# A two-layer graph network in one kernel: which product opens pass 1, and products in the last tile's waits that nothing reads

## The chip, the cores and the metric

The kernel runs on one NeuronCore of one Trainium2 chip. The metric is the device time of one execution in microseconds, lower is better; the figure given for a kernel is the median of several executions. Before the change it is 2499.7 us, the median of 3 executions (2497.94, 2499.7 and 2507.48). A profile was taken in one more execution, which took 2495.86 us; its span from the first to the last instruction is 2494.1 us, and all times inside the profile count from the start of that span.

## The reference

The input `x` has 128 graphs of 64 nodes with 768 features each; `adj` is a 0/1 matrix of 64 x 64 for each graph. Two residual layers follow each other. Everything is float32. Cut to what matters:

```python
# layer 0
h = relu(layernorm(x))
ctx = (adj @ (h @ Wadj.T + badj)) / deg + (adj.T @ (h @ Wrev.T + brev)) / rdeg + h @ Wself.T + bself
rel = (sum over j of adj[i,j] * E[rels[i,j]]) @ Wr.T + ...   # and the same for the reverse direction
x = x + ctx + rel
# layer 1: graph attention with 6 heads of 128
h = relu(layernorm(x))
hh = h @ W[head]                                     # 768 -> 6 x 128
a = leaky_relu(tanh(hh) @ w_src + (tanh(hh) @ w_dst).T)
a = softmax(where(adj == 0, -999, a))
f = elu(a @ hh + b)
g = sigmoid(h @ H_w.T + H_b)
x = x + g * f + (1 - g) * h
```

## The kernel before

Two graphs fill the 128 partitions of a tile, so there are 64 tiles (`NT`), taken in 32 pairs (`NP`). Pass 1 computes layer 0 for all pairs, one pair after the other. Pass 2 then computes layer 1 for all pairs.

The large products of a pair are a 2 x 3 by 3 x 3 product of blocks (2 tiles, 3 thirds of the features). From pair 1 on they are done with 15 block products of sums in place of 18 plain ones. Each row of the table names the left and the right factor, the PSUM bank (`a` to `d`), whether the product begins a new sum in that bank, the output block that is then read out of the bank, the sign of the reading, and whether the relation terms (`counts`) are added into the bank first:

```python
PRODUCTS = (
    ("f1", "g6", "a", True, "11", "+", False),
    ("f7", "g10", "b", True, "00", "-", False),
    ("a01", "b11", "d", True, "01", "+", True),
    ("f4", "b21", "a", False, "01", "-", False),
    ("a00", "g12", "b", False, "01", "-", False),
    ... (8 rows cut)
    ("a11", "g1", "b", False, "11", "+", True),
    ("f2", "g11", "a", False, "10", "+", True),
)
PLAIN = tuple((f"a{k}{j}", f"b{j}{q}", "abcdab"[2 * i + k], j == 0, ...   # pair 0 alone
```

In pass 1 a bank is a tile of its own with one buffer (`pwa` to `pwd` in the profile), so a product that begins a new sum in it waits until VectorE has read what stood there before. A product is six float32 matmuls of 128 x 256, shown as twelve in the profile. Behind the 15 products stands one block of relation terms alone, in bank `d`:

```python
        def main(p):
            bank = {}
            def new(b):
                bank[b] = psw.tile([P, 512], F32, name=f"pw{b}")      # psw: bufs=1
            def counts(b, c, first=False):                            # 2 bf16 matmuls (L617)
                ...
            def add(b, c, sign="+"):                                  # VectorE reads the bank
                k, q = int(c[0]), int(c[1])
                v = X[2 * p + k][:, q * CQ : (q + 1) * CQ]
                if sign == "+":
                    nc.vector.tensor_add(v, bank[b][:, :CQ], v)       # L625
                else:
                    nc.vector.tensor_sub(v, v, bank[b][:, :CQ])       # L627
            def product(an, bn, b, first, c, sign, cnt):
                ...                                                   # matmuls: L633; then counts, add
            for x in PRODUCTS if p else PLAIN:
                product(*x)

            rest_of = ["12"] if p else ["00", "10"]
            for i, c in enumerate(rest_of):
                b = "dc"[i % 2]
                steps.append(lambda b=b, c=c: (counts(b, c, True), add(b, c)))
```

Beside these steps stand, at fixed places, the other work of a pair: the sums `f1` to `f11` (the factors, formed on VectorE, L305 and L307), the preparation of the next pair, and the normalisation of the pair before. `f5`, `f6` and `f3` of a pair are formed right at its start; `f10` after 10 of its steps (six steps are one product).

In pass 2 the instructions stand in two written lists, `ORDER` for the steady part and `END` for the last pairs; each engine runs its own in that order. The parts of the attention that the change touches or that stand near it:

```python
        def rows(t):                                  # "rows": the two attention vectors, as rows
            PS[t] = pss.tile([P, 512], F32, name="ps")              # pss: three buffers
            nc.tensor.matmul(PS[t][:NR, : N + P], sdb[t % 2]..., idr, start=True, stop=True)   # L966
        def rows_dst(t):                              # "rrow"
            nc.vector.tensor_mul(rrow[t % 2][: 2 * HB], PS[t]..., de[: 2 * HB])                # L970
        def rows_src(t):                              # "lrow"
            nc.scalar.copy(lrow[t % 2][2 * HB :], PS[t][2 * HB : NR, N : N + P])               # L975
        def logits(t):                                # "log"
            PS[t] = pss.tile([P, 512], F32, name="ps")[:, : H * N].rearrange("p (h n) -> p h n", h=H)
            nc.tensor.matmul(PS[t], lrow[t % 2], rrow[t % 2], start=True, stop=True)           # L983
        def choose(t):                                # "cp": where adj, on VectorE            # L987
        def turn_p(t):                                # "turnp": 3 transposes of exp(...)      # L1014
        def attend(t):                                # "att": 24 matmuls of 64 x 128          # L1032
        def divide(t, r):                             # "ev": over the sum, into FF[t], VectorE, L1042
            if t not in FF:
                FF[t] = work.tile([P, D], F32, name="f")            # work: two buffers
        def store(t):                                 # "dma": FF[t] added into the output, from GpSimd
            nc.gpsimd.dma_start(of[t * P : (t + 1) * P, :], FF[t], accum_op=OP.add)            # L1067
```

`PG10` to `PG14` are the last five products of the last pair for the gate (half as wide as elsewhere, L1099), and `RG10` to `RG14` are their readings on VectorE (L1114, L1116). The part of `END` about them is

```python
END = """
... (cut)
pre0 f0.0/1 PG11 RG7 f0.1/1 k1 ev1.0/1 ev1.1/1 tr0 RG9 e1/1 chain1 exp0.0 rows1 f0.2/1 RG11
lrow1 rrow1 log1 swap1 exp0.1 f1.0/1 PG10 RG8 cp1 pre1 f1.1/1 tr1 turnp0 swap0 rec0 pT0 exp1.0
f1.2/1 att0 exp1.1 RG10 PG12 dma0/1 ev0.0 ev0.1 e0.0 rec1 RG12 f0.0.0 PG13 RG13 f0.1.0 e0.1
... (cut)
"""
```

where a step with `/1` belongs to the pair before the last, and a step without it to the last pair (`rows1` and `log1` are thus those of the last tile, tile 63).

Of the kernel before, what the change touches and what calls it, by code (L numbers as in the profile page):

```python
# [8 lines left out]
F32 = mybir.dt.float32  # L9
# [6 lines left out]
P = 128  # L16
# [37 lines left out]
# [6 lines that stand above are left out]
    ("f3", "g8", "c", True, "12", "-", False),  # L60
    ("a02", "g14", "a", False, "00", "-", False),
    ("f9", "g9", "b", False, "02", "+", False),
# [10 lines left out]
PLAIN = tuple((f"a{k}{j}", f"b{j}{q}", "abcdab"[2 * i + k], j == 0, f"{k}{q}" if j == 2 else None,  # L73
               "+", i > 0) for i, q in enumerate((0, 2, 1)) for k in range(2) for j in range(3))
# [58 lines left out]
def kernel(  # L133
# [45 lines left out]
    nc = tc.nc  # L179
    G, N, D = x.shape  # L180
# [5 lines left out]
    H, DO = w_src.shape  # L186
    T = G * N
    NT = T // P
    GT = P // N
    NP = NT // 2  # L190
# [35 lines left out]
    def merged(main, side):  # L226

        side = sorted(side, key=lambda e: e[0])
        i = 0
        for n, step in enumerate(main):  # L230
            while i < len(side) and side[i][0] <= n:
                side[i][1]()
                i += 1
            step()
        for _, step in side[i:]:
            step()
# [117 lines left out]
    with ExitStack() as px:  # L354
# [3 lines left out]
        pss = px.enter_context(tc.tile_pool(name="pss0", bufs=2, space=bass.MemoryType.PSUM))  # L358
# [245 lines left out]
        def main(p):  # L604

            bank = {}
            steps = []

            def new(b):
                bank[b] = psw.tile([P, 512], F32, name=f"pw{b}")  # L610

            def counts(b, c, first=False):
                k, q = int(c[0]), int(c[1])
                if first:
                    new(b)
                for i, (a, e) in enumerate(PARTS):
                    nc.tensor.matmul(bank[b][:, :CQ], CT_T[p, k][: 3 * (e - a), i, :],  # L617
                                     tabs[i][:, q * CQ : (q + 1) * CQ],
                                     start=(first and i == 0), stop=True, skip_group_check=True)

            def add(b, c, sign="+"):
# [8 lines that stand above are left out]
                def step(q, s):  # L630
                    if first and q == s == 0:
                        new(b)
                    nc.tensor.matmul(  # L633
                        bank[b][:, :CQ], OPS[p, an][:, q, s, :],
                        bw[bn][:, (s * KQ + q) * CQ : (s * KQ + q + 1) * CQ],
                        start=(first and q == s == 0), stop=(q == KQ - 1 and s == 2),
                        skip_group_check=True)
                    if q == KQ - 1 and s == 2 and c:
                        if cnt:
                            counts(b, c)  # L640
                        add(b, c, sign)
                for q in range(KQ):
                    for s in range(3):
                        steps.append(lambda q=q, s=s: step(q, s))

            for x in PRODUCTS if p else PLAIN:
                product(*x)

            rest_of = ["12"] if p else ["00", "10"]
# [3 lines that stand above are left out]
            return steps  # L653
# [144 lines left out]
        for p in range(NP):  # L798
            merged(main(p), beside(p) if p else first)
# [3 lines left out]
    with ExitStack() as px:  # L803
# [3 lines left out]
        pss = px.enter_context(tc.tile_pool(name="pss1", bufs=3, space=bass.MemoryType.PSUM))  # L807
# [24 lines left out]
        de = wb.tile([P, H, N], BF16, name="de")  # L832
        nc.gpsimd.tensor_copy(de, dl[:, :, None].to_broadcast([P, H, N]))

        idr = wb.tile([P, N + P], BF16, name="idr")
# [84 lines left out]
        def hz(t):  # L920
            return (hzs[t % NHZ][:, 0, :].rearrange("p (h o) -> p h o", h=H), hzs[t % NHZ][:, 1, :])

        TH, PR, SD, SG, PS, AM, AL, PB, DN, MX, PT, PO, FF, EE, HX = ({} for _ in range(15))
# [32 lines left out]
        def swap(t):  # L956

            hx = HX[t] = work.tile([P, H, DO], F32, name="hx")
            for g in range(GT):
                nc.sync.dma_start(hx[g * N : (g + 1) * N], hz(t)[0][(1 - g) * N : (2 - g) * N])  # L960

        def rows(t):


            PS[t] = pss.tile([P, 512], F32, name="ps")
            nc.tensor.matmul(PS[t][:NR, : N + P], sdb[t % 2].rearrange("p c v -> p (c v)")[:, :NR],  # L966
                             idr, start=True, stop=True)

# [10 lines left out]
            nc.gpsimd.memset(AM[t], NEG_MASK / LEAKY)  # L979

        def logits(t):
            PS[t] = pss.tile([P, 512], F32, name="ps")[:, : H * N].rearrange("p (h n) -> p h n", h=H)
            nc.tensor.matmul(PS[t], lrow[t % 2], rrow[t % 2], start=True, stop=True)  # L983

        def choose(t):
# [80 lines left out]
        def store(t):  # L1066
            nc.gpsimd.dma_start(of[t * P : (t + 1) * P, :], FF[t], accum_op=OP.add)  # L1067

        OF_TILE = {
            "th": tanh, "mul": multiply, "k": own_graph, "chain": split, "swap": swap, "rows": rows,  # L1070
            "rrow": rows_dst, "lrow": rows_src, "memset": fill,
            "log": lambda t: (load_x(t), logits(t)), "cp": choose, "pre": leaky, "tr": largest,
            "rec": one_over, "turnp": turn_p, "pT": copy_p, "att": attend, "g": gate, "e": exp_f,
            "dma": store,
# [161 lines left out]
```

## Time and profile before

| | us |
|---|---|
| median of 3 executions | 2499.7 |
| span of the profiled execution | 2494.1 |
| TensorE (PE) busy | 2458.7 (99%) |
| TensorE weight loads (PEld) busy | 1724.9 (69%) |
| VectorE (DVE) busy | 1998.9 (80%) |
| ScalarE (ACT) busy | 1074.4 (43%) |
| GpSimd (POOL) busy | 449.2 (18%) |
| mean granted TensorE clock | 0.998 of full speed |

A row of the chain or of a group names the line of the kernel, the engine, the operation and its operands as output<-inputs; behind it stand the times. In a list in order of time the first number is the start in us from the start of the span, the second the time taken, and a bracket at the end tells how long the engine had been idle before it and what ended that. Matmuls are pipelined: the time shown for one includes its way through the array, and the next may start before that is over, so the cost of a matmul in a row of them is read from one start to the next. Pass 1 runs from the start to about 1505 us, pass 2 from there to the end.

### The profile page before, as it was taken

The numbers are of one execution on the slowest core, as the hardware profiler recorded it, in microseconds if no ns is written. First come the engines' busy times: TensorE is split into PE (matmuls) and PEld (weight loads), VectorE is DVE, ScalarE is ACT, GpSimd is POOL, SyncE is SP. The second block draws the span as 40 slices with busy tenths as digits, with TensorE's granted clock in tenths as the row PEclk, the third lists the DMA queues.
The fourth block names the chain that finished last, engine by engine and source line by source line (L and its number), as shares of the span: only waits on it lengthen the run. The fifth ranks groups of instructions, "written<-read, shape, count | busy, mean of one in ns | idle before, by whom it ended". The sixth has DMA issues, their size and how long they took to land. (4 is left out here: it accounts for less than half of the span.)

```text
span 2494.1 us, 35435 instructions
## 1 busy us (share of the span) xinstructions
PE 2458.7 (99%) x12108; PEld 1724.9 (69%) x12108; DVE 1998.9 (80%) x4105; ACT 1074.4 (43%) x3591; POOL 449.2 (18%) x799
## 2 busy tenths in 40 slices
PE   8999999999999999999999999999999999999997
PEld 6888888888888888888888884444444444444445
DVE  8877777777777777777777766888888888888889
ACT  2122122122122222222222224777777777777777
POOL 1112112112111121121121121111111111111122
PEclk9999999999999999999999999999999999999999
DMA  5112112112122122122122154344444444444434
GB/s 178 55 53 106 53 60 100 53 66 93 54 72 87 53 74 85 53 79 81 54 88 72 53 174 140 94 110 111 109 104 110 104 104 104 107 113 105 104 85 100
DMA packets 116215, 224.58 MB, mean 90 GB/s; under 512 B 36554, under 2 KB 49981, under 8 KB 116034
## 3 DMA queue, kind: packets, MB, share of 16 engines
q1 hardware_dynamic: 106162, 197.50, 24.4%
q0 software_dynamic: 9728, 24.78, 6.2%
q8 instruction: 95, 1.56, 0.3%
q14 instruction: 86, 0.70, 0.1%
q10 hardware_dynamic: 144, 0.04, 0.0%
HBM read 96.07 MB, written 100.66 MB: 79 GB/s over the span
## 5 line engine op out<-in xcount | busy, mean ns | idle before, releaser
L633 PE MATMUL pwa<-weights,op 128*128 128x256 f32 x2304 | 548.9, 383 | 10.6 <-DVE x L625 8.8
L633 PEld LDWEIGHTS pwa<-weights,op 128*128 128x128 f32 x2304 | 417.4, 190 | 79.3 <-DVE x L625 17.3
L633 PE MATMUL pwb<-weights,op 128*128 128x256 f32 x1536 | 360.7, 381 | 0.0
L633 PEld LDWEIGHTS pwb<-weights,op 128*128 128x128 f32 x1536 | 289.1, 190 | 44.9 <-issue 6.7
L889 PE MATMUL pma<-weights,op_f 128*128 128x512 f32 x620 | 307.7, 593 | 0.6 <-DVE weights L916 0.6
L286 POOL TENSOR_TENSOR rn<-ve,mhalf 128x1 f32<-128x1 f32 x128 | 93.7, 732 | 948.6 <-DVE ve L285 948.5
L307 DVE TENSOR_TENSOR op<-op 128x768 f32<-128x768 f32 x248 | 241.3, 993 | 1.2
L941 ACT ACTIVATE pr<-pr 128x128 f32<-128x128 f32 x768 | 225.4, 296 | 25.3 <-DVE pr L931 25.2
L483 ACT ACTIVATE h<-x,rn 128x768 f32<-128x768 f32 x64 | 62.4, 1022 | 399.8 <-DVE rn L290 380.9
L663 ACT ACTIVATE hf<-x,rn 128x768 f32<-128x768 f32 x64 | 65.7, 1027 | 353.7 <-issue 250.1
L594 ACT COPY op<-pb 128x768 f32<-128x768 f32 x160 | 121.1, 797 | 180.9 <-PE pb L586 180.3
L889 PE MATMUL pmb<-weights,op_f 128*128 128x512 f32 x372 | 191.2, 595 | 0.0
L889 PEld LDWEIGHTS pma<-weights,op_f 128*128 128x128 f32 x620 | 111.8, 190 | 113.2 <-issue 104.3
L633 PE MATMUL pwc<-weights,op 128*128 128x256 f32 x780 | 187.0, 383 | 0.0
L633 PE MATMUL pwd<-weights,op 128*128 128x256 f32 x768 | 176.3, 379 | 0.0
L633 PEld LDWEIGHTS pwc<-weights,op 128*128 128x128 f32 x780 | 145.6, 190 | 25.2 <-issue 6.7
L665 POOL TENSOR_TENSOR x<-x,hf 128x768 f32<-128x768 f32 x64 | 136.1, 2127 | 134.9 <-ACT hf L663 134.9
L633 PEld LDWEIGHTS pwd<-weights,op 128*128 128x128 f32 x768 | 145.8, 190 | 20.0 <-issue 0.2
L586 PE MATMUL pb<-r,h 64*128 64x192 f32 x1536 | 151.8, 337 | 0.4 <-ACT h L483 0.4
L625 DVE TENSOR_TENSOR x<-pwa,x 128x256 f32<-128x256 f32 x95 | 40.0, 422 | 134.2 <-PE pwa L617 78.4
L586 PEld LDWEIGHTS pb<-r,h 64*128 64x128 f32 x1536 | 122.9, 187 | 33.9 <-issue 22.7
L941 ACT ACTIVATION_READ_ACCUMULATOR pr<-pr 128x1 f32 x768 | 144.4, 188 | 0.0
(207 smaller groups left out, 4337.6 us busy)
## 6 DMA issues: line engine op xcount, KB each, us to landing
x<-in_x_dram SPq DMA_DIRECT2D x64, 384.0 KB
h<-hf SPq DMA_DIRECT2D x64, 384.0 KB
out_dram<-x SPq DMA_DIRECT2D x64, 384.0 KB
hh<-hh SPq DMA_DIRECT2D x64, 384.0 KB
h<-h SPq DMA_DIRECT2D x64, 384.0 KB
x<-hh SPq DMA_DIRECT2D x64, 384.0 KB
out_dram<-f POOLq DMA_DIRECT2D x62, 384.0 KB, 5.0
hx<-weights SPq DMA_DIRECT2D x88, 192.0 KB
```

The source lines that it names most:

```text
L286: nc.gpsimd.tensor_tensor(to[:, 0:1], ve, mhalf, op=OP.pow)
L307: return (nc.vector.tensor_add if s1 == "+" else nc.vector.tensor_sub)(to, x, y)
L483: nc.scalar.activation(h, X[t], AF.Relu, scale=to[:, 0:1], bias=to[:, 1:2])
L586: nc.tensor.matmul(ps[:, g, i * 3 * N : (i + 1) * 3 * N], H0[t][s, kb * P : (kb + 1) * P], rts[p % 2][s, k].rearrange("p s n -> p (s n)"), ...
L594: nc.scalar.copy(a.rearrange("p h s (g n) -> p g (h s) n", g=GT), ps[:, :, : 6 * N].rearrange("p g (x n) -> p g x n", n=N))
L625: nc.vector.tensor_add(v, bank[b][:, :CQ], v)
L633: nc.tensor.matmul(bank[b][:, :CQ], OPS[p, an][:, q, s, :], bw[bn][:, (s * KQ + q) * CQ : (s * KQ + q + 1) * CQ], start=(first and q == s ...
L663: nc.scalar.activation(h, X[t], AF.Relu, scale=to[:, 0:1], bias=to[:, 1:2])
L665: nc.gpsimd.tensor_add(X[t], X[t], h)
L889: nc.tensor.matmul(bank[p, b], OPS[p, an][:, q, :], bw2[bn][:, 2 * q * CQ : 2 * (q + 1) * CQ], start=(first and q == 0), stop=(q == KQ - 1 ...
L941: nc.scalar.activation(PR[t][:, j, h, :], PR[t][:, j, h, :], AF.Copy, accum_out=to)
```

## The change

It has two parts, which do not depend on each other.

In pass 1, from pair 1 to pair 30, the first two products change places: the one into bank `b` comes first, the one into bank `a` second. Pair 31, the last, keeps the old order, and pair 0 has products of its own. The reason for it: the last product of a pair ends in bank `a`, and so did the next pair's first begin there.

In pass 2, for the last tile alone, TensorE gets nine products ahead of the matmul of `rows` and twelve ahead of that of `logits`, each of a bf16 identity with a constant of 384 columns, into the PSUM tile that the real matmul then overwrites. Nothing reads them. They are meant to keep TensorE working through two waits, so that its clock stays at full speed for the work behind.

```diff
-            for x in PRODUCTS if p else PLAIN:
+            later = (PRODUCTS[1], PRODUCTS[0], *PRODUCTS[2:]) if p + 1 < NP else PRODUCTS
+            for x in later if p else PLAIN:
                 product(*x)
@@
+        def keep_awake(t, n):
+            for i in range(n if t == NT - 1 else 0):
+                nc.tensor.matmul(PS[t][:, : H * N], idr[:, N:], de.rearrange("p h n -> p (h n)"),
+                                 start=True, stop=True)
+
         def rows(t):
             PS[t] = pss.tile([P, 512], F32, name="ps")
+            keep_awake(t, 9)
             nc.tensor.matmul(PS[t][:NR, : N + P], sdb[t % 2].rearrange("p c v -> p (c v)")[:, :NR],
                              idr, start=True, stop=True)
@@
         def logits(t):
-            PS[t] = pss.tile([P, 512], F32, name="ps")[:, : H * N].rearrange("p (h n) -> p h n", h=H)
+            PS[t] = pss.tile([P, 512], F32, name="ps")
+            keep_awake(t, 12)
+            PS[t] = PS[t][:, : H * N].rearrange("p (h n) -> p h n", h=H)
             nc.tensor.matmul(PS[t], lrow[t % 2], rrow[t % 2], start=True, stop=True)
```

## The prediction

> **What bounds the kernel now.** I first read the page's busy times, then who waits for whom on TensorE in pass 1, then one change of pairs in order of time.
>
> ```profile
> PE 2458.7 (99%) x12108; PEld 1724.9 (69%) x12108; DVE 1998.9 (80%) x4105; ACT 1074.4 (43%) x3591; POOL 449.2 (18%) x799
> ```
>
> TensorE is the bound nearly everywhere: 99% busy, and the next, VectorE, at 80%. A shorter pass 1 can come only from TensorE's gaps. Its waits between 100 and 1510 us are listed next (engine and line, what it waited for, us in total, times, longest), for the matmuls and for the weight loads.
>
> ```profile
> PE pwa L633 <- DVE x L625: 8.8, 30, 0.3
> PE pwa L633 <- DVE x L627: 1.7, 1, 1.7
> ...
> PEld pwa L633 <- DVE x L625: 17.3, 30, 0.6
> ```
>
> Thirty equal waits, one at each change of pairs from pair 2 to pair 31, all for VectorE's reading of bank `a`. The single wait of 1.7 us is at 1501.9, inside pair 31, which keeps its order. One change of pairs in order of time:
>
> ```profile
> 717.60 0.39 PE L617 MATMUL pwb<-tab,cntT 126*128 126x256 bf16 x2
> ...
> 718.03 0.42 DVE L625 TENSOR_TENSOR x<-pwb,x 128x256 f32<-128x256 f32 x1 [2.09 <-PE pwb L617]
> ...
> 720.81 0.38 PE L617 MATMUL pwd<-tab,cntT 126*128 126x256 bf16 x2
> 721.01 0.42 DVE L625 TENSOR_TENSOR x<-pwa,x 128x256 f32<-128x256 f32 x1 [2.56 <-PE pwa L617]
> 721.35 0.41 DVE L625 TENSOR_TENSOR x<-pwd,x 128x256 f32<-128x256 f32 x1
> ...
> 721.49 2.86 PE L633 MATMUL pwa<-weights,op 128*128 128x256 f32 x12 [0.29 <-DVE x L625]
> ```
>
> Bank `a` is read from 721.01 to 721.43, and the next pair's first product starts at 721.49. Bank `b` had been read by 718.45, over 2.5 us before it could be wanted. For what the row would look like without a wait, the only change of pairs that has none, from pair 0 to pair 1:
>
> ```profile
> 72.95 0.38 PE L617 MATMUL pwd<-tab,cntT 126*128 126x256 bf16 x2
> 73.17 0.39 PE L617 MATMUL pwc<-tab,cntT 126*128 126x256 bf16 x2
> 73.39 2.75 PE L633 MATMUL pwa<-weights,op 128*128 128x256 f32 x12
> ```
>
> A pair of relation matmuls costs 0.22 us from start to start, and the product behind it starts at once.
>
> The other part lies in the last 25 us. The columns after the stretch are its length, then busy time and instructions of PE, PEld, DVE, ACT and POOL, then TensorE's granted clock and the DMA's share and rate.
>
> ```profile
> 2470.00:2472.00 2.00, 0.16 (x1) 0.00 (x0) 2.00 (x8) 1.16 (x6) 1.32 (x6) 1.00 0.84 202
> 2472.00:2474.60 2.60, 0.28 (x1) 0.21 (x2) 2.32 (x6) 2.55 (x11) 0.21 (x1) 1.00 0.25 98
> 2474.60:2477.00 2.40, 2.36 (x8) 1.68 (x7) 2.40 (x4) 1.06 (x5) 0.69 (x1) 0.58 0.56 55
> 2477.00:2480.00 3.00, 2.43 (x30) 1.98 (x30) 2.39 (x8) 2.50 (x13) 0.87 (x1) 0.77 0.47 87
> ```
>
> TensorE idles from 2470.2 to 2474.6 but for one matmul, and then gets 0.58 and 0.77 of its clock. VectorE is busy nearly throughout. Its one stop there, in order of time:
>
> ```profile
> 2474.39 0.90 POOL L1067 DMA_DIRECT2D out_dram<-f  x1 [2.40 <-DVE weights L1114]
> ...
> 2479.45 1.64 DVE L1042 SCALAR_TENSOR_TENSOR f<-ps,dn,bb 128x128 f32<-128x128 f32 x6 [0.61 <-DMA out_dram<-f]
> ```
>
> The stop ends with a transfer: `f` has two buffers, and tile 62's division writes the one whose store (tile 60's) was issued at 2474.39.
>
> **What the skill says.** "TensorE: Matmul & The Clock Gate", part 1 (the HAM clock gate): TensorE's clock falls to half after an idle window of about 3.4 us, and rises again after as long a busy one; the window runs freely. The trace agrees in kind: 0.58 follows 4.4 us of near idleness, and in order of time the slow stretch runs from about 2474.6 to 2478, some 3.4 us. The same page, "Architectural detail", says that TensorE's queue can pull weight loads ahead of running matmuls. The trace agrees: after a change of pairs with a wait the first twelve matmuls take 2.69 us to the next product's first (721.49 to 724.18), with no wait 2.59 (73.39 to 75.98); the missing 0.10 is a weight load that stood exposed. "Perfetto Trace Analysis", "Identifying the Most-Contended Engine", warns that matmul busy time is a poor metric because matmuls are pipelined. Here 99% busy hides these waits: the 0.29 us shown as idle is only part of what one costs, which is why I read starts.
>
> **The change in pass 1.** It removes and adds no instruction. With no wait the first product would start 0.22 after 720.81, at 721.03; it starts at 721.49. So a change of pairs loses 0.46 + 0.10 = 0.56 us.
>
> - Pairs 2 to 30 now open in bank `b`, free since 718.45: 29 x 0.56 = 16.2 us gained.
> - Pair 1 loses. Pair 0's own list ends in bank `b`, and VectorE, late with the sums, reads it only from 73.34. As above (read from 721.01, product at 721.49) the product can start 0.48 later, at 73.82 in place of 73.39: 0.43, and 0.10 for the restart, 0.5 us lost.
> - Pair 31 keeps bank `a` first and its 0.56.
>
> The sum is 16.2 - 0.5 = 15.7 us, all on TensorE, which sets the end of pass 1.
>
> Does a new wait take its place? The second product now needs bank `a` at 721.03 + 2.59 = 723.62; it is free at 721.43. The fourth product needs bank `a`'s second reading. That product now ends at 726.2, VectorE is through `f10` at 726.3 (shown there in the kernel before), reads by about 726.85, and the fourth product comes at 729.59 - 0.56 = 729.03: 2.2 us spare. Bank `b`'s reading, behind the forming of `f5`, `f6` and `f3` (until 724.45), is done by 724.9 and wanted at 731.7. VectorE has 578.3 us of work in the 770 us from 700 to 1470, so 34.8 in a pair of 46.3 us; 45.7 is enough. The operand buffers turn in the old order (17 buffers, 16 taken in a pair); those of `f1` and `f7` are taken again only in the last third of the pair.
>
> Pass 2 shifts forward as a whole; from 1700 to 2300 us TensorE was busy for 600.00 of 600 us.
>
> **The change at the end.** In the changed kernel's order the nine products stand behind `PG11`, the twelve behind the matmul of `rows`. A product of 384 bf16 columns costs about 0.16 us from start to start (L983 at 2474.64, the next at 2474.80). Nine are 1.5 us, from about 2470.0 to 2471.5, and the real matmul can't start before its operand at 2472.0: 0.5 us spare. Twelve are 2.0 us, to about 2474.1, and `rrow` comes at 2474.6: 0.5 spare. Their PSUM tiles are free by then (readings ended at 2468.2 and 2471.8). So they cost nothing, and TensorE stays busy enough to keep its clock.
>
> What full speed would bring TensorE: `PG10` takes 1.57 us on the chain, 0.86 elsewhere; the three transposes behind it 0.65 or so in place of 0.33; the 24 attention matmuls about 1.2 in place of 0.8. That is 0.7 + 0.3 + 0.4 = 1.4 us. But on the path that sets the end little of it counts. The copy behind the transposes must also wait for ScalarE's work on tile 63 (until about 2476.9). The attention would end near 2478.2 in place of 2479.0, and the division behind it waits for the store until 2479.4 either way. From there VectorE runs to 2490 with stops of at most 0.33 us, in a fixed order. I take 0.1 us for this part.
>
> **The sum.** 15.7 + 0.1 = 15.8 us. From the median of 2499.7 that gives 2483.9. The profiled execution took 2495.86 and one of three 2507.48, so that the median may stand a little high; I say 2483.5.
>
> **The rivals.**
>
> 1. *The wait only moves.* VectorE reads late somewhere after the change, or another bank takes over. For it: VectorE is 80% busy, in order, and already made pair 31 wait for 1.7 us. Against it: the spare 2.2 us above, and some 10 us of VectorE's idleness in a pair. It would leave 2495 to 2500.
> 2. *The waiting part alone counts.* If only the displayed idle time of 0.29 us comes back, 28 x 0.29 = 8 us, time 2491. Against it stand the starts; it is the size to which I would fall back.
> 3. *The end counts in full.* If the store lands earlier than I think, or the executions before had the slow clock longer, 1.4 us more, time 2482.
> 4. *The unread products get in the way.* At half clock twelve would take 4 us and put off `logits` by about 1.5 us. Against it: the clock was 1.00 up to 2474.6. Time 2485.5.
>
> **Range and chances.** The mechanism of pass 1 repeats 29 times with the same numbers, so most of the width is the spread of the executions (0.4% from lowest to highest before). The range is 2477 to 2491. A gain of 2% would be 50 us, more than all of TensorE's gaps in pass 1, and a loss of 2% needs a new wait of about 1.7 us in each pair: faster 0.01, same 0.98, slower 0.01.
>
> **What would show it.** The list of TensorE's waits should have one row of about 0.3 us for bank `a` (pair 31) and one for bank `b` (pair 1) where there were thirty. A pair should take 45.74 us in place of 46.30, the last matmul of pass 1 should come near 1489 in place of 1505, and the clock should be 1.00 from 2470 to 2482 less the shift, with VectorE's stop for the store still there. I would be wrong if pairs still took 46.3, if a wait for `a` or `b` appeared at the third or fourth product, or if the span from the end of pass 1 to the end changed by over 0.5 us.

## The result, and the profile after

In the session that compares the two kernels the changed one takes 2480.08 us (median of 4 executions, 2479.78 to 2481.04) and the one before 2501.7 (4 executions, 2497.94 to 2507.48): a ratio of 0.9912 [0.9891, 0.9933]. That is within 2%, 3.4 us under the predicted 2483.5, and inside the range.

The medians differ by 21.6 us, but the two profiled executions by 2495.86 - 2480.07 = 15.8, which is the predicted sum to a tenth. So there are two questions: is each part of the 15.8 what I said it is, and where do the other 5.8 come from? The first line of the page, after:

```profile
PE 2453.2 (99%) x12129; PEld 1725.8 (70%) x12129; DVE 1998.8 (81%) x4105; ACT 1074.3 (43%) x3591; POOL 449.0 (18%) x799
```

TensorE has 21 instructions more, the unread ones, and is still the bound. Its waits for VectorE from 60 to 1500 us (engine and line, what it waited for, us in total, times, longest):

```profile
PE pwa L633 <- DVE x L627: 1.8, 1, 1.8
...
PE pwa L633 <- DVE x L625: 0.3, 1, 0.3
PE pwb L633 <- DVE x L625: 0.3, 1, 0.3
```

Thirty waits for bank `a` have become one (pair 31, old order) and one for bank `b` (pair 1). The single long wait near the end of pass 1 is still there. The same change of pairs as in the prediction, in order of time:

```profile
713.81 0.39 PE L617 MATMUL pwd<-tab,cntT 126*128 126x256 bf16 x2
...
714.01 0.42 DVE L625 TENSOR_TENSOR x<-pwa,x 128x256 f32<-128x256 f32 x1 [2.56 <-PE pwa L617]
714.03 2.75 PE L633 MATMUL pwb<-weights,op 128*128 128x256 f32 x12
...
716.62 2.75 PE L633 MATMUL pwa<-weights,op 128*128 128x256 f32 x12
...
719.42 0.42 DVE L625 TENSOR_TENSOR x<-pwa,x 128x256 f32<-128x256 f32 x1 [0.19 <-PE pwa L633]
```

The first product starts 0.22 us after the last relation matmuls and takes 2.59 to the next product, as it does where nothing waits. Bank `a`, read until 714.43, is wanted at 716.62. Its second reading ends at 719.84, and the fourth product wants it at 722.03: 2.2 us spare, the predicted figure. Over 16 pairs the same relation matmuls lie (1445.65 - 713.81) / 16 = 45.74 us apart, against (1461.61 - 720.81) / 16 = 46.30 before.

Pair 1 and the end of pass 1, in order of time on TensorE (the second part lies 1413 us later):

```profile
72.92 0.39 PE L617 MATMUL pwc<-tab,cntT 126*128 126x256 bf16 x2
73.57 2.86 PE L633 MATMUL pwb<-weights,op 128*128 128x256 f32 x12 [0.27 <-DVE x L625]
...
1485.98 2.86 PE L633 MATMUL pwa<-weights,op 128*128 128x256 f32 x12 [1.79 <-DVE x L627]
1488.67 0.39 PE L617 MATMUL pwa<-tab,cntT 126*128 126x256 bf16 x2
...
1489.12 0.38 PE L868 MATMUL ps<-ident,h 128*128 128x128 f32 x2
```

Pair 1's first product starts 0.65 after the relation matmuls in place of 0.22, a loss of 0.43, and 0.11 for the restart (2.70 to the next product in place of 2.59). The first matmul behind pass 1's products comes at 1489.12; before it came at 1505.04. Of the 15.92 us between, 0.25 were there before pair 1 began (72.92 against 73.17), so the exchange made 15.67.

The last tile, in stretches that answer to those of before, shifted with the work (columns as there):

```profile
2454.00:2456.00 2.00, 1.72 (x11) 0.78 (x8) 2.00 (x8) 1.16 (x7) 1.32 (x6) 1.00 0.84 196
2456.00:2458.70 2.70, 2.23 (x13) 1.29 (x14) 2.41 (x6) 2.65 (x11) 0.30 (x2) 1.00 0.29 109
2458.70:2461.00 2.30, 1.52 (x8) 1.12 (x7) 2.30 (x4) 1.04 (x5) 0.68 (x1) 1.00 0.51 41
2461.00:2464.00 3.00, 2.46 (x31) 2.13 (x32) 2.46 (x8) 2.57 (x13) 0.87 (x1) 1.00 0.53 99
```

TensorE is busy in the first two, and the granted clock (the first column behind POOL's) is 1.00 in all four, where before it was 0.58 and 0.77 in the last two. In order of time on TensorE, and then VectorE's stop:

```profile
2454.09 1.63 PE L969 MATMUL ps<-de,idr 128*128 128x384 bf16 x9
2456.13 0.28 PE L977 MATMUL ps<-idr,sdb 128*82 128x192 bf16 x1 [0.42 <-POOL sdb L955]
2456.25 2.11 PE L969 MATMUL ps<-de,idr 128*128 128x384 bf16 x12
2458.73 0.32 PE L996 MATMUL ps<-rrow,lrow 82*128 82x384 bf16 x1 [0.37 <-DVE rrow L981]
2458.89 1.03 PE L1112 MATMUL pmb<-weights,op_f 128*128 128x256 f32 x4
```

```profile
2463.47 1.64 DVE L1055 SCALAR_TENSOR_TENSOR f<-ps,dn,bb 128x128 f32<-128x128 f32 x6 [0.54 <-DMA out_dram<-f]
```

The unread products end 0.42 and 0.37 us before the operands of the real ones come, `PG10` takes 0.86 us to the next start (the transposes, at 2459.75) in place of 1.53 (2476.33 - 2474.80 before; the prediction's 1.57 is the chain's figure), and VectorE still stops for the store of tile 60. (The rows with x9 and x12 are the unread products; the real matmul follows each.) From 1489.12 to the end these two profiles take 989.18 us, against 989.06 from 1505.04 before. So in them the second part brought nothing, as predicted. The experiments show that this holds for these two profiles only.

### The profile page after: what moved, and what is told of

Its sections match the earlier page's. It is cut to its first block, busy times and chain, and to the rows that moved or that the text cites. A ratio compares the mean times of both kernels' runs of the same rounds, so it can differ in the third digit from the quotient of the medians.

```text
span 2478.3 us, 35477 instructions
## 1 busy us (share of the span) xinstructions
PE 2453.2 (99%) x12129; PEld 1725.8 (70%) x12129; DVE 1998.8 (81%) x4105; ACT 1074.3 (43%) x3591; POOL 449.0 (18%) x799
```

## The experiments

**What is to be told apart.** Theory A (mine): the exchange is worth 15.7 us by the starts, and the end next to nothing. Its first rival: only the displayed idle time counts, 8 us. The second: the end is worth 1 to 2 us, because executions differ in where the slow clock falls, and the one that I read was a lucky one. The third asks for the other 5.8 us: something in the change that the profiles don't show, or differences between executions in places that the change doesn't touch.

Each time below is the median of a kernel's executions, with lowest, highest and number; each ratio is to the kernel before in the same session, where that took 2500.45 (23 executions, 2496.49 to 2504.63), 2498.81 (11) and 2499.09 (16). The record names another chip for each of these three sessions, so a kernel is compared with the one before in its own session.

**The kernel before against itself.** No edit.

> The kernel before itself, for its spread and for one more profile. Theory A (all of the gain lies in 29 changes of pairs, and the rest of the difference of the medians, 21.6 against 15.8 in the profiles, is spread of the kernel before between executions): the profiled span is again 2494 to 2496 us, or, if it is one of the longer executions, the extra time is found in one place that has nothing to do with the change of pairs. Theory C (in other executions VectorE's reading of bank a comes later than in the profiled one, so the change of pairs costs more than 0.56): a longer execution shows waits for bank a of over 0.3 us.

2502.14 us (2495.91 to 2504.39, 12), ratio 1.0004 [0.9994, 1.0014]. Its profiled execution took 2503.52, 7.7 us longer than that in the prediction, with the same instructions. The first place where they part is the start, on TensorE in order of time; first this execution, then the one in the prediction:

```profile
11.34 2.85 PE L458 MATMUL pb<-wrt,es 128*81 128x384 f32 x4
...
18.47 3.68 PE L633 MATMUL pwa<-weights,op 128*128 128x256 f32 x8
```

```profile
10.88 1.52 PE L458 MATMUL pb<-wrt,es 128*81 128x384 f32 x4
...
14.62 1.99 PE L633 MATMUL pwa<-weights,op 128*128 128x256 f32 x8
```

Every matmul takes nearly twice as long, until about 22 us, with no wait between. Pair 0's last relation matmuls in bank `b` come at 78.26 in place of 72.72: 5.54 us lost. (The views show the granted clock as 1.00 here in both, because the trace has no record of it ahead of its first rise. That first record, at full speed, begins at 21.91 us here and at 10.55 in the prediction's profile, which agrees with the durations.) The second place is the last tile. Stretches as above, then three stops of VectorE in order of time:

```profile
2478.30:2480.50 2.20, 0.00 (x0) 0.10 (x1) 1.91 (x5) 2.15 (x12) 0.23 (x1) 0.77 0.26 103
2480.50:2483.00 2.50, 2.48 (x8) 1.93 (x7) 2.50 (x5) 1.04 (x5) 0.68 (x1) 0.50 0.55 61
2483.00:2486.00 3.00, 2.43 (x27) 1.75 (x26) 2.12 (x6) 2.47 (x13) 0.88 (x1) 0.50 0.44 80
...
2489.00:2490.00 1.00, 1.00 (x6) 0.91 (x5) 0.69 (x2) 0.07 (x1) 0.00 (x0) 0.63 0.00 0
```

```profile
2485.59 1.64 DVE L1042 SCALAR_TENSOR_TENSOR f<-ps,dn,bb 128x128 f32<-128x128 f32 x6 [0.88 <-PE ps L1032]
...
2487.60 0.42 DVE L1116 TENSOR_TENSOR weights<-weights,pma 128x256 f32<-128x256 f32 x1 [0.27 <-PE pma L1099]
...
2489.31 0.42 DVE L1114 TENSOR_TENSOR weights<-pmb,weights 128x256 f32<-128x256 f32 x1 [0.82 <-PE pmb L1099]
```

The same wait of TensorE, but the slow clock starts before the work comes and lasts longer: a clock of 0.77 in the first stretch is half speed for 46% of it, so from 2479.5, and 0.63 in the last is full speed for its last 26%, so until 2489.7. `PG10`, the transposes, the attention, `PG12` and `PG13` all lie in these 10.2 us. VectorE stops for TensorE three times, 1.97 us in all, where in the prediction's profile it stopped for the store alone. From the start of `PG11` (2475.01) to the start of VectorE's last two instructions (2496.90) it takes 21.89 us, there 20.10. The waits for bank `a` are the same 30 of 0.3 us, 8.8 in all, so theory C, a later reading in the longer executions, doesn't hold. Theory A wanted the extra time in one place; it lies in two, and 0.3 us of it in a third, below.

**The exchange alone.** `keep_awake` makes nothing.

> Only the exchange of the first two products, no unread products at the end. Theory A: span 2478.3 +- 0.3, time 2480 to 2482, within 1 us of the changed kernel; TensorE's clock in the last 20 us falls again as it did before. Theory B (the unread products bring the 6 us by which the medians differ more than the profiles): time about 2486.

```diff
-            for i in range(n if t == NT - 1 else 0):
+            for i in range(0):
```

2484.62 us (2483.27 to 2489.86, 4), ratio 0.9941 [0.9926, 0.9956]: 15.8 us under the session's median of before. That is neither theory A's 2480 to 2482 nor theory B's 2486, so the time alone decides nothing; the profile does. The last tile took 21.85 us, with the clock at 0.50 from 2461 to 2470, as in the kernel before against itself. Against the changed kernel's 20.03 the lack of the unread products cost 1.8 us here. The profile showed a third place where executions differ, the wait near the end of pass 1: 3.10 us where the changed kernel's profile has 1.79, and the twelve matmuls behind it 4.38 to the next start in place of 2.69, at half clock.

**The end alone.** The old order in all pairs, with the unread products.

> Only the unread products, the old order of products. Theory A: span within 0.3 us of 2494.1 in a profile of the same kind, clock 1.00 through the last tile, no change of the time beyond the spread of the kernel before. Theory B: about 6 us less than the kernel before. A third possibility, that the end counts in full: 1.4 us less in the span.

```diff
-            later = (PRODUCTS[1], PRODUCTS[0], *PRODUCTS[2:]) if p + 1 < NP else PRODUCTS
+            later = PRODUCTS
```

2499.47 us (2495.76 to 2503.87, 12), ratio 0.9993 [0.9984, 1.0002]. By the medians alone this can't be told from nothing: the executions lie 8 us apart. The profile tells it, the last tile took 19.81 us. It also has the pass-1 wait at its worst, on TensorE in order of time:

```profile
1503.23 5.49 PE L633 MATMUL pwa<-weights,op 128*128 128x256 f32 x12 [3.04 <-DVE x L627]
1508.52 0.63 PE L617 MATMUL pwa<-tab,cntT 126*128 126x256 bf16 x2
```

These twelve matmuls take 5.29 us from start to start.

**All pairs but pair 1.** Pair 1 keeps the old order, pair 31 gets the new one.

> The changed kernel, but pair 1 has the old order and pair 31 the new one. Theory A: pair 1 gets its 0.5 us back (no wait for bank b at its start). Pair 31 loses its wait of 0.3 us at the start, but further on VectorE waits for loads of the weights of pass 2 and TensorE for VectorE (1.8 us near the end of pass 1), so that the 0.56 us saved there comes back as a longer wait of 2.3 us. Sum: span 0.5 us below the changed kernel's 2478.3. If pair 31 counts too: 1.1 us below.

```diff
-            later = (PRODUCTS[1], PRODUCTS[0], *PRODUCTS[2:]) if p + 1 < NP else PRODUCTS
+            later = (PRODUCTS[1], PRODUCTS[0], *PRODUCTS[2:]) if p > 1 else PRODUCTS
```

2484.75 us (2482.85 to 2487.87, 4), ratio 0.9939 [0.9924, 0.9953]. This was a miss on my side, and it shows what pair 31's exception is for. Pair 31 on TensorE:

```profile
1445.59 2.75 PE L633 MATMUL pwb<-weights,op 128*128 128x256 f32 x12
1448.18 0.59 PE L633 MATMUL pwa<-weights,op 128*128 128x256 f32 x2
1451.68 2.43 PE L633 MATMUL pwa<-weights,op 128*128 128x256 f32 x10 [2.91 <-DMA weights<-in_w_cat_dram]
```

In the last pair the first weights of pass 2 are loaded at its seventh step, into the place of `g6`, which by then has been read if `f1` x `g6` is the first product. As the second it reads the new weight: TensorE waits 2.91 us for the load, and pair 31's blocks are computed with a replaced factor. The time is to be read with that. Pair 1 itself starts without a wait there (73.17, then 73.39), as in the kernel before. Up to the end of pair 30, which the replaced factor doesn't touch, this profile has the 29 changed openings by themselves: the last relation matmuls of pair 30 come at 1445.37 us, in the prediction's profile at 1461.61, and those of pair 0 in the same bank `d` at 72.95 in both. That is 16.24 us, 0.56 for each.

**The changed kernel against itself**, in a second session. No edit.

> The changed kernel again, beside the two next ones. By the profiles so far three stretches differ between executions by the phase of TensorE's clock: the first 25 us (the first products run at half clock for up to 5 us longer), the wait near the end of pass 1 (1.7 to 3.1 us, and after the long ones 12 products at half clock, up to 2.6 us more), and, without the unread products, the last tile (20.1 or 21.9 us from the last product before the wait to VectorE's last instruction; 19.8 to 20.0 with them). So the time is 2479 to 2488 from execution to execution, ratio to the kernel before 0.993, that is 15.7 us of pass 1 and 1 to 1.8 of the end. If it is 2480 throughout, ratio 0.991, the exchange calms more than the end.

2488.05 us (2482.88 to 2488.84, 6), ratio 0.9947 [0.9933, 0.9960]. So the same kernel that took 2479.8 to 2481.0 before takes up to 8 us more here, and the difference of medians is 10.8 us in place of 21.6. The profiled execution (2483.64) had the pass-1 wait at 3.42 us and 4.38 for the twelve matmuls, 3.3 us more than in the first profile, and its usual start (72.92). Four others took 2487.7 to 2488.8; they were not profiled, and which place made them long is not shown.

**Three sums later.** The wait near the end of pass 1 is VectorE's: in pair 31 it forms sums of pass 2's weights, some of which wait for loads, and it takes its instructions in order. On VectorE, changed kernel, in order of time:

```profile
1480.51 2.48 DVE L307 TENSOR_TENSOR weights<-weights 128x1024 f32<-128x1024 f32 x2 [1.35 <-DMA weights<-in_hw_t_dram]
...
1485.51 0.41 DVE L627 TENSOR_TENSOR x<-x,pwa 128x256 f32<-128x256 f32 x1
```

The reading at 1485.51, for which TensorE waits, stands behind them. The edit moves three of them back, so that the two that stood ahead of this reading stand behind it:

> The changed kernel; in pair 31 three sums of weights of pass 2 (g1, g8, g11) stand on VectorE behind the readings of banks a and b that they stood in front of. If the wait of 1.7 to 3.1 us near the end of pass 1 is VectorE's order (the readings stuck behind sums that wait for loads), it goes, and with it the half clock after it: 1.7 us less in a good execution, 2.5 to 4 less in the median. If the loads themselves set the end of pass 1, the wait moves to the first products of pass 2 and the time is unchanged.

```diff
-                    (59, "g5"), (65, "v"), (67, "g3"), (70, "g9"), (73, "g1"), (76, "g8"),
-                    (79, "g11"))])
+                    (59, "g5"), (65, "v"), (67, "g3"), (70, "g9"), (78, "g1"), (84, "g8"),
+                    (84, "g11"))])
```

2479.03 us (2478.07 to 2484.44, 6), ratio 0.9918 [0.9904, 0.9933]. The wait fell to 0.55 us, with the clock kept:

```profile
1490.28 2.86 PE L633 MATMUL pwa<-weights,op 128*128 128x256 f32 x12 [0.55 <-DVE x L627]
```

How long the wait is, a load decides. VectorE's last sum ahead of the readings waits for a part of `hw_t` to land, 1.3 to 3.5 us in the profiles, and TensorE's wait follows it. With the sums in their old place it is 0.42 to 0.45 us longer than VectorE's in seven of eight profiles (from 1.33 and 1.75 in the prediction's to 2.99 and 3.42 in the changed kernel's second); the eighth, the exchange alone, has 2.38 and 3.10. With the three sums later it is 1.4 to 1.8 us shorter than VectorE's: 1.94 leaves 0.55 here, and in kernels below 2.67 leaves 1.14 and 3.46 leaves 1.71. So the edit shortens the wait and takes it away only when the load comes early. Why the load lands later in one execution than in the next is not shown.

The executions fall into two groups, 2478.1 to 2479.5 (four) and 2483.9 to 2484.4 (two). The median is 9.0 us under that of the changed kernel in the same session; that is more than this wait can give, and the changed kernel's four long executions are in it. The profiled one is of the second, and its matmuls at the start ran at half speed as in the kernel before against itself: pair 0's relation matmuls came at 78.46, 6 us later than the changed kernel's 72.47.

**Unread products at the start.** Sixteen small ones ahead of TensorE's first matmul and fifteen ahead of its next group, into PSUM tiles that the real ones then overwrite.

> The changed kernel; TensorE gets 16 unread products before its first one and 15 in its second wait (2.4 to 6.4 us from the start), which the real ones then overwrite. If the spread of the start (pair 1 begins at 72.4 to 78.3 us) is the clock's window, the clock is up by 9 us in each execution: pair 1 begins at 71 to 72.5 us, and the longest executions lose up to 5.5 us, the median 1 to 3. If loads set the start, nothing changes.

```diff
@@ ahead of TensorE's first matmul
-            ds = pss.tile([P, 2, 512], F32, name="pb")[:, 0, : 4 * N].rearrange(
-                "p (k d n) -> p k d n", k=2, d=2)
+            pb = pss.tile([P, 2, 512], F32, name="pb")
+            for i in range(0 if p else 16):
+                nc.tensor.matmul(pb[:, 0, :P], blkb, blkb, start=True, stop=True)
+            ds = pb[:, 0, : 4 * N].rearrange("p (k d n) -> p k d n", k=2, d=2)
@@ ahead of the first table product
+                for j in range(15):
+                    nc.tensor.matmul(TAB["ps"][:, 0, :P], blkb, blkb, start=True, stop=True)
```

2480.81 us (2479.72 to 2482.40, 5), ratio 0.9923 [0.9910, 0.9936]. The start on TensorE:

```profile
2.36 1.89 PE L520 MATMUL pb<-blkb 128*128 128x128 bf16 x16 [2.36 <-DVE blkb L404]
...
4.40 1.80 PE L457 MATMUL pb<-blkb 128*128 128x128 bf16 x15
6.71 2.82 PE L460 MATMUL pb<-wrt,es 128*81 128x384 f32 x4 [0.50 <-DVE mv L283]
...
10.77 1.52 PE L460 MATMUL pb<-wrt,es 128*81 128x384 f32 x4
```

The clock is not up by 9 us, as I had expected it to be: its first record begins at 10.24 us, and in the four kernels below with the same products at 6.08 to 7.66. They don't make the start shorter than its good case (72.62 for the relation matmuls). They may keep the bad one away: no execution of this kernel, nor of the four below that have these products too, was in the upper group; only profiled ones show the start itself, and all five profiles have it at 72.3 to 72.6.

**All of it together.** The changed kernel with both of these and the old order in pair 1.

> The changed kernel with the unread products at the start, the three sums later, and the old order in pair 1. If the spread is TensorE's clock in the three places and nothing else, all executions lie within 1.5 us of each other: pair 1 begins at 72.5 us with no wait for bank b (0.5 us less than the changed kernel), the wait near the end of pass 1 is under 0.6 us, the last tile takes 20.0. Time 2477 to 2478, ratio to the kernel before 0.991. If other places vary too, the spread stays at 4 us or more.

```diff
-            later = (PRODUCTS[1], PRODUCTS[0], *PRODUCTS[2:]) if p + 1 < NP else PRODUCTS
+            later = (PRODUCTS[1], PRODUCTS[0], *PRODUCTS[2:]) if 1 < p < NP - 1 else PRODUCTS
```

2477.85 us (2476.99 to 2479.02, 4), ratio 0.9915 [0.9899, 0.9930]. Two microseconds from lowest to highest, where I had said 1.5. Pair 1 starts without a wait, and the product near the end of pass 1 with 0.2 us of one (0.43 us behind the relation matmuls in place of 0.22):

```profile
72.94 0.38 PE L621 MATMUL pwc<-tab,cntT 126*128 126x256 bf16 x2
73.17 2.75 PE L637 MATMUL pwa<-weights,op 128*128 128x256 f32 x12
...
1483.19 0.39 PE L621 MATMUL pwb<-tab,cntT 126*128 126x256 bf16 x2
1483.62 2.86 PE L637 MATMUL pwa<-weights,op 128*128 128x256 f32 x12
```

This kernel, whose executions agree within these two microseconds, is the ground on which the two parts were measured by medians. Each was taken out of it.

**The end taken out**: `keep_awake` makes nothing, as in the exchange alone.

> As e6_all without the unread products in the last tile. The only noise left is then the last tile's clock. My theory as corrected by the profiles so far (a loss of 0 to 1.8 us according to the window's phase): 0.5 to 1.8 us over e6_all in the median, and in the profile the last stretch is 20.1 or 21.9. The theory on record in the prediction (0.1 us): no difference.

2480.17 us (2478.26 to 2481.40, 4), ratio 0.9923 [0.9909, 0.9936]: 2480.17 - 2477.85 = 2.3 us more. With four executions each, whose ranges overlap (by 2478.26 against 2479.02), the size is rough. It is also not the end's alone. The profiles are 3.58 us apart, and the last tile makes 1.84 of that (22.10 us against 20.26); most of the rest is the wait near the end of pass 1, which is back although the three sums stand later. VectorE, then TensorE:

```profile
1481.93 2.49 DVE L307 TENSOR_TENSOR weights<-weights 128x1024 f32<-128x1024 f32 x2 [3.46 <-DMA weights<-in_hw_t_dram]
...
1485.13 2.86 PE L637 MATMUL pwa<-weights,op 128*128 128x256 f32 x12 [1.71 <-DVE x L631]
```

So the 1.84 us of the last tile are what this pair of profiles shows for the end's products.

**The exchange taken out**: `later = PRODUCTS`, as in the end alone.

> As e6_all, but with the old order of the first two products in all pairs: the exchange by itself with little noise about it. 29 changes of pairs of 0.56 us: 16.2 us over e6_all. If what the list of waits shows as idle (0.29) were all: 8.5 us.

2494.14 us (2493.16 to 2495.04, 12), ratio 0.9976 [0.9968, 0.9985]: 2494.14 - 2477.85 = 16.3 us for 29 pairs. Its waits from 60 to 1500 us:

```profile
PE pwa L637 <- DVE x L629: 8.8, 30, 0.3
```

The displayed 8.8 us are back, less the 0.3 that pair 31 has in both, and the time is 16.3 us longer. The 8 us of the rival are refuted. The 16.3 have some of the pass-1 wait in them, though (1.14 us in this profile, 0.2 in that of all together). From pair 0's last relation matmuls in bank `b` to pair 31's, which leaves out the start, the end of pass 1 and the last tile, it is 1498.97 - 72.37 = 1426.60 us here and 1483.19 - 72.50 = 1410.69 there: 15.91. The 0.33 that lack to 16.24 were lost in pair 2, where VectorE waited 1.83 us for a load (`bb`), so that bank `a` was read late once.

**The store's stop taken away.** The output of tile 62 goes into a buffer of another pool, so that the division doesn't wait for the store of tile 60.

> As e6_all, but the division of tile 62 writes another buffer, so that it doesn't wait for the store of tile 60. If that store is what holds VectorE for 0.5 us in the last tile, the stop goes and the end comes 0.5 us earlier, 2476.5 to 2477.5. If TensorE's attention products hold it as well, it stays.

```diff
-                FF[t] = work.tile([P, D], F32, name="f")
+                FF[t] = (keep.tile([P, D], F32, name="fx", tag="x", bufs=6) if t == NT - 2 else
+                         work.tile([P, D], F32, name="f"))
```

2477.45 us (2476.72 to 2478.20, 4), ratio 0.9912 [0.9899, 0.9926]. The stop, 0.77 us in the profile of all together, is gone, on VectorE:

```profile
2459.90 0.40 DVE L1134 TENSOR_TENSOR weights<-weights,pmb 128x256 f32<-128x256 f32 x1
2460.23 1.62 DVE L1060 SCALAR_TENSOR_TENSOR fx<-ps,dn,bb 128x128 f32<-128x128 f32 x6
```

The last tile takes 19.42 us in place of 20.26, but the median moved by only 0.4, within the spread of either; what of the 0.8 an average execution gains is left open. Its median is the lowest of the study, and all its executions lie below all ten of the changed kernel (2479.78 at the lowest), though in another session.

**The sum over the profiles.** If three places and the exchange are all that differs, the terms, each read from a kernel's own profile, must add up to its time. Against the prediction's profile (2495.86): the start is the time of pair 0's last relation matmuls in bank `b`; the exchange is the stretch from these to pair 31's last ones in bank `b`; the wait is the stretch from there to the first product of pass 2, so that the wait near the end of pass 1 and the matmuls at half clock behind it lie within; the tile is from `PG11` to the start of VectorE's last two instructions.

| kernel | start | exchange | wait | last tile | adds up to | measured |
|---|---|---|---|---|---|---|
| before against itself | +5.54 | -0.01 | +0.33 | +1.79 | 2503.5 | 2503.52 |
| exchange alone | -0.35 | -15.71 | +3.03 | +1.75 | 2484.6 | 2484.68 |
| end alone | +0.05 | 0.00 | +4.17 | -0.29 | 2499.8 | 2499.77 |
| changed, first profile | -0.25 | -15.71 | +0.04 | -0.07 | 2479.9 | 2480.07 |
| changed, second | +0.20 | -15.71 | +3.36 | -0.16 | 2483.6 | 2483.64 |
| three sums later | +5.74 | -15.71 | -1.42 | -0.08 | 2484.4 | 2484.44 |
| start's products | -0.10 | -15.72 | +0.66 | -0.01 | 2480.7 | 2480.87 |
| all together | -0.22 | -15.91 | -1.92 | +0.16 | 2478.0 | 2477.82 |
| all, no end | -0.30 | -15.99 | -0.26 | +2.00 | 2481.3 | 2481.40 |
| all, old order | -0.35 | 0.00 | -0.83 | -0.28 | 2494.4 | 2494.35 |
| all, store's stop away | -0.38 | -16.04 | -1.97 | -0.68 | 2476.8 | 2476.72 |

Each agrees within 0.2 us. The exchange is the one term without a spread: 15.71 or 15.72 in all five profiles in which pair 1 takes part, 0.00 or 0.01 in the three with the old order, and 15.91 to 16.04 in the three with the loss in pair 2. (All pairs but pair 1 is left out: it has the wait for a load besides.)

## Why the prediction was right, and where it was not

- **"The sum is 16.2 - 0.5 = 15.7 us" in pass 1**: right. Between the two profiles 15.67 at the first matmul of pass 2, and 15.71 up to pair 31 in five profiles; the 29 pairs by themselves 16.24 in one profile. The pair's 45.74 us, the two waits left and pass 1's end near 1489 came as said. That the displayed idle time is half of what a wait costs, the step from 0.29 to 0.56 us, holds.
- **Pair 1 loses 0.5**: right, 0.43 + 0.11. It needn't be lost: with the old order pair 1 has no wait (0.20 to 0.33 us of it were lost again in pair 2 in three profiles, and nothing in a fourth).
- **No new wait (rival 1)**: right; the 2.2 us spare at the fourth product were measured as 2.2.
- **The unread products cost nothing (rival 4)**: right; 0.42 and 0.37 us spare against the 0.5 and 0.5 that I worked out.
- **"I take 0.1 us for this part"**: this is the step that failed. In the two profiles that I had or got first it holds, 20.10 and 20.03 us. But it rests on one execution, in which the slow clock lasted from 2475 to 2478.4 and ran out in the middle of the attention, ahead of all of `PG12` and `PG13`. In the three other profiles without the products (before against itself, exchange alone, all but the end) the last tile took 21.85 to 22.10, in all eight with them (the one with tile 62 in another buffer left out) 19.8 to 20.3. So the path that I had wrong is VectorE's, which I held to wait for the store either way. In those three it waited for TensorE's half-speed products: it read `PG13` 14.30 us behind the start of `PG11` in each, and 12.73 and 12.66 in the first two. (In the exchange alone the store landed late besides, a stop of 1.21 us, and `PG13` still came last.) The term is 1.8 to 2.0 us in these three, and nothing in the one that I read. That the sum of 15.8 met the two first profiles to a tenth was luck: both had the short start, nearly the same wait near the end of pass 1, and that of before the one short last tile. The clause that I wrote beside rival 3, "or the executions before had the slow clock longer", was right; its other reason, a store that lands earlier, was not needed.
- **"The median may stand a little high"**: right in kind, too small. I took 0.4 us off the median. Against the profiled execution the session's median of before stood 5.8 us high, and the changed kernel's median at its profile. That is the other 5.8 us of the 21.6. The second session gave 10.8 with the same two kernels. Two places that the change doesn't touch move an execution, by up to 5.7 us at the start and up to 4.2 at the wait near pass 1's end, and with four executions a median can fall on either side. Which of them made each unprofiled execution long is shown in part only. In the end alone three long executions (2501.45 to 2502.35) have a mean granted clock of 0.999 on record, the same as the shortest four (up to 2497.67), so no slow stretch that the clock's record holds made them long, and the slow start, which it doesn't hold, is the one of the known places that fits. For the changed kernel's four at 2487.7 to 2488.8 (0.998) it decides nothing. That mending both brings the spread from some 8 us (twelve executions of before) to 1.5 to 3.1 in the four kernels that have both speaks for these two.

"TensorE: Matmul & The Clock Gate" of the Trainium skill, part 1, says that the clock's window runs freely and doesn't start with the kernel, and that the same kernel therefore shows different numbers of slow matmuls from run to run. I had cited that page and yet read the slow clock from a single execution. The runs agree with it: one kernel, one wait in the last tile, 3.4 us of half clock in one execution and 10.2 in the next.

## What to carry to other kernels

A wait that recurs at every turn of a loop is to be costed from start to start, here 0.56 us where 0.29 were shown as idle, and then multiplied with confidence. A cost that hangs on TensorE's clock after a pause of some microseconds is a matter of phase: one profile can show it as nothing, so look at two or three executions before calling it nothing. Where the executions of one kernel spread more than the change is worth, mend the places that spread them first and measure the change on that ground, or read it from a stretch of the profiles that the spread doesn't reach: from pair 0 to pair 31 the profiles of the kernel before agreed within 0.01 us, while their times lay 7.7 us apart.

## What was not expected of the hardware

**The slow clock comes in whole multiples of some 3.4 us.** In the prediction's profile, by the two stretches shown there, 0.84 x 2.4 + 0.46 x 3.0 = 3.4 us at half speed. In the kernel before against itself 10.2 us, above, and so in the two other profiles without the end's products. Near the end of pass 1 of the end alone, one stretch (columns as above):

```profile
1500.00:1520.00 20.00, 16.10 (x46) 8.92 (x45) 13.06 (x31) 4.83 (x11) 6.68 (x20) 0.83 0.43 146
```

0.34 x 20 = 6.8 us. The traces' records of the granted clock give these stretches as 3.41, 6.83 and 10.24 us. So one, two and three times 3.4, which fits a window of that length. How many it is goes with the moment at which the slow stretch begins. In all seven that lie amid work, those that began after TensorE had started again took one (2474.98 against 2474.64 in the prediction's profile; two more near the end of pass 1), and those that began before it took two or three (2479.50 against 2480.52 in the kernel before against itself; three more). The busy share of a window doesn't decide it: TensorE was busy for 2.84 of the 3.41 us before the clock rose in the prediction's profile, and for 2.85 and 2.86 of 3.4 where it did not rise (the second windows of the exchange alone and of all, no end). What decides is not shown.

**The length of a pause doesn't settle it alone.** Near the end of pass 1 waits of 0.55 to 2.38 us left the clock full, and 3.04, 3.10 and 3.42 us brought 5.29, 4.38 and 4.38 us for the twelve matmuls in place of 2.69: the longest of these is not the longest wait. With the first the slow clock began before the product did (1502.27 against 1503.23), with the other two behind its start.

**The start is slower than the page says.** In the kernel before against itself TensorE worked from 9.76 us on without a wait, and at half speed until about 22, over 12 us; "TensorE: Matmul & The Clock Gate", part 1, gives some 3.4 us of sustained work for the rise. In the prediction's profile the rise came at 10.55, by the first record of the clock. No run explains it.
